# Row LSTM on one core: the even pixels' gate product moved to GpSimd, and a new written order of the half-step

## The chip, the core and the metric

The kernel runs on one core of a Trainium2 chip. The metric is device time in microseconds (us); the median of three runs of the kernel before is 2024.15 us (2023.83 to 2025.46).

## The reference

An input x of 8 images, 96 channels, 128 rows and 128 columns is group-normalised (32 groups). The normalised image goes through a masked 1x3 convolution to 384 gate channels. Then the rows are walked from top to bottom as time steps of a convolutional LSTM, and the result is added to x:

```python
def step(carry, row_in):
    h, c = carry
    ss = conv1d(h, W_ss, padding=1) + b_ss      # width 3, 96 -> 384 channels
    gates = ss + row_in
    f, i, o = sigmoid(gates[0]), sigmoid(gates[1]), sigmoid(gates[2])
    g = tanh(gates[3])
    c_new = f * c + i * g
    h_new = o * tanh(c_new)
    return (h_new, c_new), h_new
...
x = x + conv_lstm(group_norm(x))
```

All of it is float32. Row r+1 can't begin before h of row r is there, so the 128 rows are one long chain.

## The kernel before, in words

**Two chains.** The 8 images are two streams s of 4 images each. A half-step n is one row of one stream (n = 2 row + s), 256 half-steps in all. The streams don't depend on each other, so work of half-step n fills the waits of n-1. Rows come in blocks of R = 4.

**Statistics first.** The first 140 us or so read all of x and make means and scales (VectorE's bn_stats, ScalarE's sums). The loop over half-steps follows, from `do(n, PERIOD, by_lanes=True)` (L937).

**Products.** Columns are held as even and odd pixels, t = 0 and 1 (called a and b in the written order), 256 columns each for four images. The width-3 convolution is done with sums and differences of neighbours: `vs` = even + odd (L573), `vf` = odd - even (L585), both on VectorE with two SBUF inputs, and `vd`, the differences with the shifted neighbour (L589, GpSimd). The gate channels are three tiles A, B, C of 128: 96 rows of a sigmoid gate (A forget, B input, C output) and 32 rows of the tanh gate. Each tile has a PSUM bank of 512 columns, even and odd half. Eight banks go round. Products of the input's own convolution are P, Q, E (from `xs`), those of h are 1 (vs), 2 (vf), 0 and 3 (vd). In the loop TensorE works as two row groups of 64 rows, called lanes; each of 1, 2, 0, 3 is written twice, once for each lane, so a half-step has 33 products. Where two lanes write the same bank one after the other, a wait is put between them (`Lanes.wait`, L394).

**After the products.** 1 and 2 go to the two halves of the bank; ScalarE copies the first with the bias (`cp`, L508), VectorE writes their sum (`lo`, even, L512) and difference (`hi`, odd, L516) back; products 3, E and 0 are then added on top. A matmul on a bank waits for the last VectorE write to that bank, whichever half it is in. Then ScalarE does sigmoid (`si`, L527) and tanh (`ta`, L520), VectorE the forget product (`fg`, L532), the gate product i * g (`gt`, L537), the cell sum (`ce`, L547), ScalarE tanh of c (`th`, L552), VectorE the output h (`ou`, L560), from which vf (`F`) and vs (`S`) of the stream's next row come.

**GpSimd** makes vd (`D`, L589), adds h to x (`re`, L607), and prepares later rows: `own_image` widens one image's rows from `xr` to `xw` (L297), and makes the sum (L315) and the differences (L316) into `xs`; `normalise_shared` writes the rows shared with h's tile (L297 too). `vd` carries a manual wait for the last of `vf` and `vs`.

**What sets the order.** The engines' queues are filled by hand: the string `PERIOD` (L678) is read name by name for every half-step n, and each name issues one instruction in its engine's queue. A quote mark after a name means half-step n-1, two mean n-2, a plus n+1; `F'` and `S'` make the operands of n+1 from h of n-1; a small a or b at the end means the even or odd pixels alone. `W` stands for `prepare(n - 1)`: own image, shared rows and row loads (SP's queue) of the half-step before. `FIRST` (L629) is what the first eight half-steps prepare. Within an engine, work runs in this order only.

```python
PERIOD = (
    "2A hiC' siA' D'' 1B 1A taA' 2B fg' 3C' 1A 0C' re'' taB' 2A 2B EC' 1B cpA 0C' 2C W loA cpB "
    "3C' 1C siB' loB PB+ QA+ hiA taCb' 2C hiB taCa' 0A gtb' 1C siC' gta' EA 0B ceb' cpC 3A PA+ "
    "cea' thb' PC+ 3B loC tha' QC+ oub' EB oua' QB+ 3A F' 3B 0A S' 0B"
)
```

Of the kernel before, what the change touches and what calls it, by code (L numbers as in the profile page):

```python
# [8 lines left out]
AF = mybir.ActivationFunctionType  # L9
# [6 lines left out]
def strided(ap, offset, dims):  # L16

    return bass.AP(ap.tensor, ap.offset + offset, [ap.ap[0], *[list(d) for d in dims]])
# [3 lines left out]
def kernel(  # L22
# [32 lines left out]
    nc = tc.nc  # L55
    B, C, H, W = x.shape
    P = 128
    NH = 2
    BH = B // NH
    R = 4  # L60
    NB = H // R
    J = W // 2
# [53 lines left out]
    def pair(shape, name):  # L116
        return [
            [const.tile(shape, F32, tag=f"{name}{s}{i}", name=f"{name}{s}{i}") for i in range(2)]
            for s in range(NH)
        ]  # L120
# [5 lines left out]
    xs = pair([P, R, 3, BH, J], "xs")  # L126
# [4 lines left out]
    xw = [const.tile([P, R, W + 1], F32, tag=f"xw{i}", name=f"xw{i}") for i in range(2)]  # L131
# [29 lines left out]
    E = mybir.EngineType  # L161
# [147 lines left out]
            s * BH + j,  # L309
        )  # L310

    def combine(xw, n, total, differences):

        e, o = xw[:, 0:n, 0:J], xw[:, 0:n, J + 1 :]
        nc.gpsimd.tensor_add(total, e, o)  # L315
        nc.gpsimd.tensor_sub(  # L316
            differences,
            strided(xw[:, 0, :], 0, [(W + 1, n), (J, 2), (1, J)]),
            strided(xw[:, 0, :], J + 1, [(W + 1, n), (0, 2), (1, J)]),
        )  # L320

    def own_image(s, k, j):

        to = xs[s][k % 2]
        widen(nc.gpsimd, xw[0], 0, R, s, k, j, 0)
        combine(xw[0], R, to[:, :, 0, j, :], to[:, :, 1:3, j, :])

    def own_row(xw, s, r, lo=0, hi=BH):

        to = xs[s][0]  # L330
        combine(
            xw[:, lo:hi],
            hi - lo,
            to[:, r, 0, lo:hi],
            to[:, r, 1:3, lo:hi].rearrange("p t b j -> p b t j"),
        )
# [19 lines left out]
    HB = BH * J  # L356
    NT = NB * R
    last = NT * NH - 1
# [49 lines left out]
    class HalfStep:  # L408


        def __init__(self, n):
            self.n, (self.row, self.s) = n, divmod(n, NH)
            self.ps, self.m1, self.moving, self.done, self.gates, self.th = {}, {}, {}, set(), None, None
            self.started, self.images, self.halves, self.writer = set(), {}, {}, {}
            self.hx = hx[self.s][self.row // R % 2][:, self.row % R]
            self.xs = xs[self.s][self.row // R % 2][:, self.row % R]
            self.c = cs[self.s].rearrange("p t b j -> p (t b j)")
# [34 lines left out]
        def own(self, a, i):  # L452

            low = a == order["A"] or (a == order["C"] and (self.s == 0 or (self.n, i) == (1, 2)))
            rhs = self.xs[:, i].rearrange("p b j -> p (b j)")
            self.mm(a, i % 2, wo[i], rhs, slice(0, C2) if low else slice(C2, P))
# [63 lines left out]
            nc.scalar.activation(self.part(g, lo, hi, t), self.part(ps, lo, hi, t), AF.Tanh)  # L520


        def sigmoid(self, a):
            if self.row == 0 and a == 0:
                return
            gate = self.ps[a][0:C]
            nc.scalar.activation(gate, gate, AF.Sigmoid)  # L527

        def forget(self):
            f = self.ps[0][0:C]  # L530
# [3 lines left out]
        def gated(self, lo=0, hi=BH, t=None):  # L534
            to = self.g if self.row > 0 else self.c
            to, i, g = (self.part(ap, lo, hi, t) for ap in (to, self.ps[1][0:C], self.g))
            nc.vector.tensor_mul(to, i, g)  # L537


        def part(self, ap, lo, hi, t=None):  # L540
            ap = ap.rearrange("p (t b j) -> p t b j", t=2, b=BH)
            return ap[:, :, lo:hi] if t is None else ap[:, t, lo:hi]
# [44 lines left out]
        def shifted(self, lo=0, hi=BH):  # L587
            h = self.hx[:, 0, lo, :]
            diff = nc.gpsimd.tensor_sub(  # L589
                self.operand("vd", 2)[:, :, lo:hi],  # L590
                strided(h, 1, [(BH * JP - 1, 2), (JP, hi - lo), (1, J)]),
                strided(h, 0, [(BH * JP + 1, 2), (JP, hi - lo), (1, J)]),
            )
            if self.last.ins.engine != E.Pool:
                tc.add_manual_dep(
                    diff.ins,
                    self.last.ins.name,
                    mybir.DependencyInfo(
                        mybir.DependencyClass.Sync, mybir.DependencyReason.SCHED_ONLY
                    ),  # L600
                    reason="GpSimd starts when VectorE is done with both SBUF reads",
                )

        def residual(self):
            s, row = self.s, self.row
            xo = xt[s, row // R][0:C, :, row % R, :].rearrange("p b (j t) -> p t b j", t=2)
            (nc.gpsimd if 2 * row + s < last else nc.vector).tensor_add(xo, xo, self.h)  # L607

    def store(s, k, lo, hi):
        nc.sync.dma_start(  # L610
# [7 lines left out]
    SHARED = (((0, 0, R), (3, 0, 1)), ((1, 0, R),), ((2, 0, R),), ((3, 1, R),))  # L618
# [4 lines left out]
    def shared(s, k, *images):  # L623
        return [
            (normalise_shared, nc.gpsimd, s, k, *(j if isinstance(j, tuple) else (j, 0, R)))
            for j in images
        ]

    FIRST = [  # L629
        own(0, 0),  # L630
        own(0, 1),
        own(0, 2) + shared(0, 1, 0, 1),
        own(0, 3) + [(load_rows, 0, 2)] + shared(0, 1, 2, 3),
        own(1, 0, 1),
        own(1, 2) + shared(1, 1, 0, 1),
        own(1, 3) + [(load_rows, 1, 2)] + shared(1, 1, 2, 3),
        [(own_image, 0, 2, 0), (own_image, 1, 2, 0)],
    ]

    def work(n):  # L640
        if n < len(FIRST):
            return FIRST[n]
        row, s = divmod(n, NH)
        k, r = divmod(row, R)
        parts = []
        if r == R - 1 and k + 2 < NB:
            parts.append((own_image, s, k + 2, 0))
        elif r < R - 1 and k + 1 < NB:
            parts.append((own_image, s, k + 1, r + 1))
        if k + 1 < NB:  # L650
            parts += shared(s, k + 1, *SHARED[r])
        if r == R - 2 and k + 2 < NB:
            parts.append((load_rows, s, k + 2))
        return parts

    worked = set()

    def prepare(n):
        if n not in worked:
            worked.add(n)  # L660
            for part, *args in work(n):
                part(*args)

    def finish(n):
        prepare(n)
# [10 lines left out]


    PERIOD = (  # L678
        "2A hiC' siA' D'' 1B 1A taA' 2B fg' 3C' 1A 0C' re'' taB' 2A 2B EC' 1B cpA 0C' 2C W loA cpB "
        "3C' 1C siB' loB PB+ QA+ hiA taCb' 2C hiB taCa' 0A gtb' 1C siC' gta' EA 0B ceb' cpC 3A PA+ "  # L680
        "cea' thb' PC+ 3B loC tha' QC+ oub' EB oua' QB+ 3A F' 3B 0A S' 0B"
    )
    PIXELS = {"a": (0, BH, 0), "b": (0, BH, 1)}
    SPLIT = ("taC", "gt", "ce", "th", "ou")
    PARTS = {
# [5 lines left out]
    steps = {}  # L691

    def half_step(n):
        if n not in steps:
            steps[n] = HalfStep(n)
        return steps[n]

    def do(n, names, by_lanes=False):

        for name in names.split():  # L700
            if name == "W":
                prepare(n - 1)
                continue
            at = n
            for mark, offset in (("'", -1), ("+", 1), ("*", 2)):
                at += offset * name.count(mark)
                name = name.replace(mark, "")
            pixels = PIXELS[name[-1]] if name[:-1] in SPLIT and name[-1] in PIXELS else ()
            whole_name = name[:-1] if pixels else name
            tile_ = whole_name[-1] if whole_name[-1] in order else ""  # L710
            part = whole_name[: len(whole_name) - len(tile_)]

            if part in ("S", "F", "D"):
                at += NH
            if not 0 <= at <= last:
                continue
            step = half_step(at)
            if name in step.done or whole_name in step.done:
                continue
            if by_lanes and (part in OWN or part in H_PRODUCTS) and (  # L720
                at < last or part in ("P", "Q") or (part, order[tile_]) in step.halves
            ):
                if step.piece(part, order[tile_]):
                    step.done.add(name)
                continue
            step.done.add(name)
            getattr(step, PARTS[part])(*([order[tile_]] if tile_ else []), *pixels)
            if by_lanes and part == "re":
                finish(at)
# [13 lines left out]
    late = []  # L743
# [106 lines left out]
    n = m = 0  # L850
    for b in range(B):
# [7 lines left out]
        for k in range(QW // CH):  # L859
# [11 lines left out]
            if alone:  # L871
                i = list(shares).index(k)
# [25 lines left out]
    j = BH - 1  # L898
# [104 lines left out]
```

## Time and profile before

| | us |
|---|---|
| median of three runs | 2024.15 |
| profiled execution | 2027.04 |
| its span | 2025.2 |
| one half-step in the loop (vf to vf) | 7.33 |
| TensorE busy in the span | 1923.3 |
| VectorE busy | 1529.1 |
| ScalarE busy | 1494.9 |
| GpSimd busy | 1473.1 |

In the profile PE is TensorE (a matmul of 64 rows is two records of 0.38 us), PEld its weight load, DVE is VectorE, ACT is ScalarE, POOL is GpSimd, SP issues the DMAs. A line of the timeline gives start and length in us, engine, source line, operation, output and input, sizes, and a count where several equal instructions follow each other. Idle time before an instruction stands in brackets with what ended it. An engine's busy time is the time in which at least one of its instructions is running.

### The profile page before, as it was taken

How to read it: one execution, taken by the hardware profiler on the slowest of the kernel's cores; microseconds unless marked ns; L12 is line 12 of the kernel's file. 1: busy time of each engine (PE TensorE's matmuls, PEld its weight loads, DVE VectorE, ACT ScalarE, POOL GpSimd, SP SyncE). 2: the span in 40 equal slices, each digit the busy share in tenths (PEclk: the TensorE clock that was granted, in tenths of full speed). 3: DMA queues.
4: the chain of work that ended last, by engine and by line, in shares of the span. 5: the costliest groups of instructions: out<-in, count | busy, mean ns of one | idle time of the engine just before them, and what ended most of it. 6: DMA issues, size and time to landing. Idle time of an engine off the chain costs nothing.

```text
span 2025.2 us, 44842 instructions
## 1 busy us (share of the span) xinstructions
PE 1923.3 (95%) x16936; PEld 1831.0 (90%) x16936; DVE 1529.1 (76%) x3996; ACT 1494.9 (74%) x3161; POOL 1473.1 (73%) x1712
## 2 busy tenths in 40 slices
PE   0289999999999999999999999999999999999998
PEld 0178999999999999999999999999999999999997
DVE  5767777777777777777777777777777777777776
ACT  3776777777777777777777777777777777777776
POOL 3348777777777777777777777777777777777752
PEclk9989999999999999999999999999999999999999
DMA  9994333444334334433433443343344333434411
GB/s 374 424 310 100 98 103 91 112 115 104 82 89 113 92 101 115 113 83 82 110 95 95 116 116 95 79 100 96 93 116 116 96 82 96 107 92 106 116 33 32
DMA packets 103382, 237.11 MB, mean 117 GB/s; under 512 B 5952, under 2 KB 8896, under 8 KB 97280
## 3 DMA queue, kind: packets, MB, share of 16 engines
q1 hardware_dynamic: 103168, 234.25, 42.0%
q8 instruction: 135, 2.21, 0.5%
q14 instruction: 79, 0.65, 0.1%
HBM read 183.90 MB, written 50.33 MB: 116 GB/s over the span
## 4 chain that ended last, share of the span: by engine, by line
PE 93%; DMA 4%; ACT 2%; DVE 1%; issue 0%; SPq 0%; POOL 0%; DVEq 0%; POOLq 0%
PE ps L442 92%; DMA piece<-in_x_dram 3%; DMA xs<-in_x_dram 1%; ACT piece L216 1%; PE ps L174 0%; ACT piece L217 0%; DVE bst L876 0%; ACT hx L295 0%; ACT piece L295 0%; DVE hx L560 0%; ACT xs L216 0%; ACT xs L217 0%; SPq L864 0%; PE pv L251 0%; DVE ps L516 0%
## 5 line engine op out<-in xcount | busy, mean ns | idle before, releaser
L442 PE MATMUL ps<-vd,wl 64*128 64x256 f32 (+1 forms) x6096 | 1390.9, 379 | 0.3
L442 PEld LDWEIGHTS ps<-vd,wl 64*128 64x128 f32 (+1 forms) x6096 | 1028.4, 186 | 45.7 <-issue 2.4
L442 PE MATMUL ps<-vs,wm 64*128 64x256 f32 (+1 forms) x3052 | 775.1, 380 | 4.9 <-POOL vs L573 4.4
L442 PE MATMUL ps<-vf,wm 64*128 64x256 f32 (+1 forms) x3052 | 766.3, 377 | 0.0
L527 ACT ACTIVATE ps<-ps 96x512 f32<-96x512 f32 x766 | 441.6, 577 | 356.2 <-PE ps L442 348.1
L442 PE MATMUL ps<-xs,wx 64*128 64x256 f32 x3080 | 637.8, 377 | 11.1 <-POOL xs L315 11.1
L589 POOL TENSOR_TENSOR vd<-hx 128x512 f32<-128x512 f32 x257 | 266.7, 1038 | 388.5 <-PE ps L442 384.8
L442 PEld LDWEIGHTS ps<-xs,wx 64*128 64x128 f32 x3080 | 494.0, 187 | 14.2 <-POOL xs L315 11.6
L520 ACT ACTIVATE g<-ps 32x256 f32<-32x256 f32 (+1 forms) x1021 | 468.6, 482 | 26.7 <-PE ps L442 6.3
L442 PEld LDWEIGHTS ps<-vf,wm 64*128 64x128 f32 (+1 forms) x3052 | 475.4, 187 | 11.0 <-PE ps L442 0.4
L442 PEld LDWEIGHTS ps<-vs,wm 64*128 64x128 f32 (+1 forms) x3052 | 459.6, 186 | 21.6 <-POOL vs L573 5.4
L512 DVE TENSOR_TENSOR ps<-m,ps 128x256 f32<-128x256 f32 x768 | 326.0, 425 | 192.5 <-ACT m L508 182.0
L442 PE MATMUL ps<-xs,wt 64*128 64x256 f32 x1530 | 453.2, 377 | 0.6 <-DVE ps L516 0.6
L508 ACT ACTIVATE m<-ps,wl 128x256 f32<-128x256 f32 x766 | 361.6, 474 | 90.9 <-PE ps L442 84.3
L532 DVE TENSOR_TENSOR ps<-ps,c 96x512 f32<-96x512 f32 x254 | 176.8, 696 | 232.9 <-PE ps L442 226.9
L607 POOL TENSOR_TENSOR x<-x,hx 96x512 f32<-96x512 f32 x255 | 330.8, 1297 | 6.7 <-DVE hx L560 6.7
L516 DVE TENSOR_TENSOR ps<-m,ps 128x256 f32<-128x256 f32 x768 | 300.8, 422 | 1.3 <-PE ps L442 1.2
L442 PEld LDWEIGHTS ps<-xs,wt 64*128 64x128 f32 x1530 | 280.0, 186 | 12.8 <-DVE ps L516 1.0
L316 POOL TENSOR_TENSOR xs<-xw 128x512 f32<-128x512 f32 (+1 forms) x254 | 270.9, 1067 | 0.0
L297 POOL TENSOR_SCALAR hx<-x,rstd,nmr 32x384 f32<-32x384 f32 (+2 forms) x312 | 225.8, 724 | 33.2 <-DMA x<-in_x_dram 1.1
L297 POOL TENSOR_SCALAR xw<-xr,rstd,nmr 128x512 f32<-128x512 f32 x252 | 205.6, 816 | 7.1 <-DVE nmr L289 6.5
L537 DVE TENSOR_TENSOR g<-ps,g 96x256 f32<-96x256 f32 x507 | 189.0, 413 | 3.8 <-ACT g L520 3.8
(91 smaller groups left out, 1223.1 us busy)
## 6 DMA issues: line engine op xcount, KB each, us to landing
xr<-in_x_dram SPq DMA_DIRECT2D x124, 512.0 KB, 6.4
x<-in_x_dram SPq DMA_DIRECT2D x63, 768.0 KB, 6.1
out_dram<-x SPq DMA_DIRECT2D x62, 768.0 KB, 4.6
xs<-in_x_dram SPq DMA_DIRECT2D x30, 1024.0 KB, 12.3
piece<-in_x_dram SPq DMA_DIRECT2D x16, 1024.0 KB, 12.3
x<-in_x_dram SPq DMA_DIRECT2D x62, 256.0 KB, 3.2
xs<-in_x_dram SPq DMA_DIRECT2D x4, 512.0 KB, 8.7
out_dram<-x SPq DMA_DIRECT2D x2, 576.0 KB, 3.7
```

The costliest lines, as they stand in the source:

```text
L297: return engine.tensor_scalar(dst, src, scale, shift, ALU.mult, ALU.add)
L316: nc.gpsimd.tensor_sub(differences, strided(xw[:, 0, :], 0, [(W + 1, n), (J, 2), (1, J)]), strided(xw[:, 0, :], J + 1, [(W + 1, n), (0, 2) ...
L442: made = nc.tensor.matmul(self.ps[a][:, bass.ts(half, HB)][:, cols], weights[rows, bass.ts(a, P)], rhs[rows, cols], start=new, stop=False, ...
L508: nc.scalar.activation(self.m1[a], m1, AF.Identity, bias=column)
L512: nc.vector.tensor_add(self.ps[a][:, 0:HB], self.m1[a], self.ps[a][:, HB:])
L516: nc.vector.tensor_sub(hi, self.m1[a], hi)
L520: nc.scalar.activation(self.part(g, lo, hi, t), self.part(ps, lo, hi, t), AF.Tanh)
L527: nc.scalar.activation(gate, gate, AF.Sigmoid)
L532: nc.vector.tensor_mul(f, f, self.c)
L537: nc.vector.tensor_mul(to, i, g)
L589: diff = nc.gpsimd.tensor_sub(self.operand("vd", 2)[:, :, lo:hi], strided(h, 1, [(BH * JP - 1, 2), (JP, hi - lo), (1, J)]), strided(h, 0, ...
L607: (nc.gpsimd if 2 * row + s < last else nc.vector).tensor_add(xo, xo, self.h)
```

## The change

Five edits:

1. The sigmoid of tile B is done in two halves. The odd half stays in PSUM; the even half is written to a new SBUF tile `i`. The gate product of the even pixels reads that tile and runs on GpSimd; the odd pixels' product stays on VectorE.
2. `PERIOD` is written anew. Sigmoid A is issued at the end of its own half-step, tanh B, the first half of sigmoid B and tanh A ahead of the copies; odd A comes directly after even A; products P and E of later use are ahead of 0A.
3. What a half-step prepares is split in three places: U (first half-steps only), V (shared rows, right after the residual) and W (own image and row loads). W now stands after the gate product `gta'`, so on GpSimd the own image comes after it.
4. The residual on GpSimd gets the same manual wait for the stream's next vs as vd has.
5. The first eight half-steps do five of their shared-row normalisations on ScalarE, and two own images of stream 1 are cut in three parts that go to different half-steps (`apart`, `LATER`).

```diff
-        def sigmoid(self, a):
+        def sigmoid(self, a, lo=0, hi=BH, t=None):
             if self.row == 0 and a == 0:
                 return
-            gate = self.ps[a][0:C]
-            nc.scalar.activation(gate, gate, AF.Sigmoid)
+            gate = self.part(self.ps[a][0:C], lo, hi, t)
+            if t == 0:
+                self.even_input = self.tile("i", (C, HB))
+                to = self.even_input.rearrange("p (b j) -> p b j", b=BH)
+            else:
+                to = gate
+            nc.scalar.activation(to, gate, AF.Sigmoid)
...
-            nc.vector.tensor_mul(to, i, g)
+            if t == 0 and self.even_input is not None:
+                i = self.even_input.rearrange("p (b j) -> p b j", b=BH)
+                nc.gpsimd.tensor_mul(to, i, g)
+            else:
+                nc.vector.tensor_mul(to, i, g)
...
-            if self.last.ins.engine != E.Pool:
+            self.hold(diff)
+
+        def hold(self, made):
+            if self.last is not None and self.last.ins.engine != E.Pool:
                 tc.add_manual_dep(
-                    diff.ins,
+                    made.ins,
...
-            (nc.gpsimd if 2 * row + s < last else nc.vector).tensor_add(xo, xo, self.h)
+            made = (nc.gpsimd if 2 * row + s < last else nc.vector).tensor_add(xo, xo, self.h)
+            following = steps.get(self.n + NH)
+            if self.n < last and following is not None:
+                following.hold(made)
...
+    def on_scalar(s, k, *images):
+        return [(normalise_shared, nc.scalar, s, k, j, 0, R) for j in images]
+
+    def apart(s, k, j):
+        to = xs[s][k % 2]
+        return (
+            (widen, nc.gpsimd, xw[1], 0, R, s, k, j, 0),
+            (add_pixels, xw[1], R, to[:, :, 0, j, :]),
+            (subtract_pixels, xw[1], R, to[:, :, 1:3, j, :]),
+        )
+
+    spread = apart(1, 1, 0)
     FIRST = [
-        own(0, 0),
-        own(0, 1),
-        own(0, 2) + shared(0, 1, 0, 1),
-        own(0, 3) + [(load_rows, 0, 2)] + shared(0, 1, 2, 3),
-        own(1, 0, 1),
-        own(1, 2) + shared(1, 1, 0, 1),
-        own(1, 3) + [(load_rows, 1, 2)] + shared(1, 1, 2, 3),
-        [(own_image, 0, 2, 0), (own_image, 1, 2, 0)],
+        ([], [], own(0, 0)),
+        ([], [], own(0, 1)),
+        ([], [], own(0, 2)),
+        (on_scalar(0, 1, 0), [spread[0]], own(0, 3) + [(load_rows, 0, 2)]),
+        (on_scalar(0, 1, 1), list(spread[1:]), own(1, 1)),
+        (on_scalar(0, 1, 2) + on_scalar(1, 1, 2), shared(0, 1, 3), own(1, 2)),
+        (on_scalar(1, 1, 3), shared(1, 1, 0, 1), own(1, 3) + [(load_rows, 1, 2)]),
+        ([], [], [(own_image, 0, 2, 0)]),
     ]
+    LATER = dict(zip((11, 13, 15), apart(1, 2, 0)))
...
+        early, late = shared(s, k + 1, *SHARED[r]) if k + 1 < NB else [], []
+        if n in LATER:
+            early.append(LATER[n])
+        ahead, image = (k + 2, 0) if r == R - 1 else (k + 1, r + 1)
+        if ahead < NB:
+            late.append((own_image, s, ahead, image))
         if r == R - 2 and k + 2 < NB:
-            parts.append((load_rows, s, k + 2))
-        return parts
+            late.append((load_rows, s, k + 2))
+        return [], early, late
...
     PERIOD = (
-        "2A hiC' siA' D'' 1B 1A taA' 2B fg' 3C' 1A 0C' re'' taB' 2A 2B EC' 1B cpA 0C' 2C W loA cpB "
-        "3C' 1C siB' loB PB+ QA+ hiA taCb' 2C hiB taCa' 0A gtb' 1C siC' gta' EA 0B ceb' cpC 3A PA+ "
-        "cea' thb' PC+ 3B loC tha' QC+ oub' EB oua' QB+ 3A F' 3B 0A S' 0B"
+        "2A 1B 1A U taB' 2B 3C' siBa' 1A 0C' taA' 2A 2B EC' fg' 1B cpA D'' re'' V 0C' 2C siBb' "
+        "loA 3C' cpB 1C hiA PB+ QA+ taCb' loB 2C taCa' PA+ gtb' 1C gta' W siC' EA hiB PC+ ceb' 0A "
+        "cpC cea' 0B 3A thb' loC 3B tha' QB+ oub' 3A oua' EB 0A F' 0B QC+ S' siA 3B hiC"
     )
-    SPLIT = ("taC", "gt", "ce", "th", "ou")
+    SPLIT = ("taC", "siB", "gt", "ce", "th", "ou")
```

`combine` is only cut into `add_pixels` and `subtract_pixels`, which it calls; on the built program's GpSimd queue a half-step reads vd, residual, shared rows, gate product, widen, sum, differences.

More of the change, by code (lines that the diff above doesn't have):

```diff
@@ L310, in widen, with add_pixels, subtract_pixels @@
         )
-    def combine(xw, n, total, differences):
-        e, o = xw[:, 0:n, 0:J], xw[:, 0:n, J + 1 :]
-        nc.gpsimd.tensor_add(total, e, o)
+    def add_pixels(xw, n, total):
+        nc.gpsimd.tensor_add(total, xw[:, 0:n, 0:J], xw[:, 0:n, J + 1 :])
+    def subtract_pixels(xw, n, differences):
         nc.gpsimd.tensor_sub(
@@ L320, in combine @@
         )
+    def combine(xw, n, total, differences):
+        add_pixels(xw, n, total)
+        subtract_pixels(xw, n, differences)
     def own_image(s, k, j):
@@ L414, in __init__ @@
             self.started, self.images, self.halves, self.writer = set(), {}, {}, {}
+            self.even_input = self.last = None
             self.hx = hx[self.s][self.row // R % 2][:, self.row % R]
@@ L644, in work, with prepare @@
         k, r = divmod(row, R)
[L645 to L651, printed above, removed]
+        early, late = shared(s, k + 1, *SHARED[r]) if k + 1 < NB else [], []
[4 more added lines that the diff above has]
+            late.append((own_image, s, ahead, image))
         if r == R - 2 and k + 2 < NB:
-            parts.append((load_rows, s, k + 2))
-        return parts
+            late.append((load_rows, s, k + 2))
+        return [], early, late
     worked = set()
[L658 to L662, printed above, removed]
+    def prepare(n, parts=(0, 1, 2)):
+        for i in parts:
+            if (n, i) not in worked:
+                worked.add((n, i))
+                for part, *args in work(n)[i]:
+                    part(*args)
     def finish(n):
@@ L700, in do @@
         for name in names.split():
-            if name == "W":
-                prepare(n - 1)
+            if name in "UVW":
+                prepare(n - 1, range("UVW".index(name) + 1))
                 continue
```

## The prediction

> **What bounds the kernel now.** I read the page's busy shares and chain first, then the busy time by stretches of 200 us, then the timeline of one half-step engine by engine.
>
> ```profile
> PE 1923.3 (95%) x16936; PEld 1831.0 (90%) x16936; DVE 1529.1 (76%) x3996; ACT 1494.9 (74%) x3161; POOL 1473.1 (73%) x1712
> ...
> PE 93%; DMA 4%; ACT 2%; DVE 1%; issue 0%; SPq 0%; POOL 0%; DVEq 0%; POOLq 0%
> ```
> ```profile
> 400.00:600.00 200.00, 200.00 (x1803) 192.26 (x1802) 152.94 (x408) 150.44 (x327) 154.24 (x170) 1.00 0.39 98
> ```
>
> TensorE looks full, but busy is the union of two row-group lanes: one lane may sit idle unseen. In the timeline a lane takes a record every 0.216 us (1004.12, 1004.34, 1004.55, 1004.77). A half-step has 33 products of two records each, over two lanes: 33 x 0.216 = 7.12 us. It takes 7.33 (vf at 1000.97 and 1008.30). The 0.21 missing is seen here, VectorE's timeline and then TensorE's:
>
> ```profile
> 1000.97 0.42 DVE L585 TENSOR_TENSOR vf<-hx 128x256 f32<-128x256 f32 x1
> 1001.31 0.42 DVE L573 TENSOR_TENSOR vs<-hx 128x256 f32<-128x256 f32 x1
> ...
> 1004.39 0.90 DVE L512 TENSOR_TENSOR ps<-m,ps 128x256 f32<-128x256 f32 x2 [0.70 <-ACT m L508]
> 1005.20 0.76 DVE L516 TENSOR_TENSOR ps<-m,ps 128x256 f32<-128x256 f32 x2
> ...
> 1007.52 0.74 DVE L560 TENSOR_TENSOR hx<-ps,th 96x256 f32<-96x256 f32 x2
> 1008.30 0.42 DVE L585 TENSOR_TENSOR vf<-hx 128x256 f32<-128x256 f32 x1
> ```
> ```profile
> 1004.99 0.63 PE L442 MATMUL ps<-xs,wx 64*128 64x256 f32 x4
> 1005.42 0.59 PE L442 MATMUL ps<-vf,wm 64*128 64x256 f32 x2
> 1005.77 0.45 PE L442 MATMUL ps<-vd,wl 64*128 64x256 f32 x1
> ```
>
> The vd product (0A) waits for odd A (L516, first of the pair, done at 1005.62), which stands behind even A and even B. One lane is empty from 1005.46 to 1005.77. So the bound is a loop: last product on A, copy A, even A, even B, odd A, 0A. TensorE alone would be 3% faster.
>
> GpSimd's timeline over the same half-step shows when the SBUF port is free:
>
> ```profile
> 1001.90 1.04 POOL L589 TENSOR_TENSOR vd<-hx 128x512 f32<-128x512 f32 x1 [1.55 <-PE ps L442]
> 1002.90 1.30 POOL L607 TENSOR_TENSOR x<-x,hx 96x512 f32<-96x512 f32 x1
> 1004.18 0.81 POOL L297 TENSOR_SCALAR xw<-xr,rstd,nmr 128x512 f32<-128x512 f32 x1
> 1005.07 0.65 POOL L315 TENSOR_TENSOR xs<-xw 128x256 f32<-128x256 f32 x1
> 1005.67 1.07 POOL L316 TENSOR_TENSOR xs<-xw 128x512 f32<-128x512 f32 x1
> 1006.85 0.82 POOL L297 TENSOR_SCALAR hx<-x,rstd,nmr 32x512 f32<-32x512 f32 x1
> ```
>
> It is done at 1007.67, 0.63 us before the next vf. The idle 1.55 before vd is put down to a TensorE product; vd also waits for vs, which ends 0.17 before it (1001.73 to 1001.90). That gap is what keeps vf and vs alone on the port. Early in the run it is missing (timelines of VectorE, GpSimd, TensorE at 160 us):
>
> ```profile
> 160.45 0.43 DVE L585 TENSOR_TENSOR vf<-hx 128x256 f32<-128x256 f32 x1
> 160.79 1.29 DVE L573 TENSOR_TENSOR vs<-hx 128x256 f32<-128x256 f32 x1
> ```
> ```profile
> 160.46 1.34 POOL L316 TENSOR_TENSOR xs<-xw 128x512 f32<-128x512 f32 x1
> ```
> ```profile
> 162.13 0.70 PE L442 MATMUL ps<-vs,wm 64*128 64x256 f32 x3
> ```
>
> vf wins the port, the subtraction L316 waits for it (1.34 for 1.07) and then keeps vs out until 162.08, 1.63 after vf's start where 0.76 is usual. Products on vs start at 162.13. The same happens at 200.66, and the next vf comes 8.11 later, not 7.33.
>
> **What the Trainium skill says.** "SBUF — State Buffer", "Who interferes with whom": a VectorE instruction with two SBUF inputs contends with a GpSimd instruction that reads SBUF; the first takes the port for its whole length, the other blocks. The trace agrees, with the 1.29 us above. One SBUF input beside PSUM doesn't contend: agreed, L315 keeps to 0.64 under VectorE's PSUM operations. "GPSIMD Engine Reference", "Engine selection": two-input elementwise work is about twice as slow on GpSimd as on VectorE. Here it is 0.64 against 0.42 for 128x256, and I use the trace.
>
> **The change part by part.**
>
> Order of products: 0A moves from 19th to 23rd of 33, and odd A stands right behind even A. Odd A comes one VectorE slot (0.34) earlier and 0A four product slots (4 x 0.216 = 0.86) later, so the 0.31 wait goes. Worth up to 0.21 per half-step.
>
> Sigmoid B in two halves: ScalarE gets two 96x256 at about 0.41 (L552's size) for one 96x512 of 0.58, +0.2; it has over 1.5 us free per half-step. Nothing on the path.
>
> Even gate product (L537, first in time for the odd pixels, second for the even): VectorE loses one 0.33 slot; GpSimd gains 96x256, not shown there: its nearest row is L315, 0.64; upper end 0.73, the longer of its two 128x256 differences before the loop; I take 0.64. It waits for the even half of tanh C. Behind it on GpSimd stand, by the built program's order, the own image (L297, L315, L316) and then the next vd. For it waits the cell sum of the even pixels, and behind that on VectorE the output, vf and vs.
>
> The own image is so moved from before the gate to after it. GpSimd now runs vd, residual, shared rows, [wait] gate, own image: 1.04+1.30+0.81+0.64+2.6 = about 6.4 us, and vd can't start until 0.17 after vs ended. Counted from vs's end (0):
> - 1B starts at 0.05 (162.08 to 162.13). From it to the second 3C' are 13 products: six rounds of two lanes, 6 x 0.43, and the last of 0.59: 3.18. Sum 3.23.
> - tanh C in two halves 0.65 and a 0.04 wait: 3.92. A GpSimd wait is 0.08 (L297's end at 1004.99 to L315 at 1005.07): gate 4.00 to 4.64.
> - Even cell, tanh, output 3 x 0.41, and four waits of 0.035: vf is ready at 6.01, or up to 0.14 later if the odd pixels' instructions hold it: 6.08.
> - GpSimd: own image starts at 4.60 (its back-to-back overlap is 0.04), the subtraction L316 1.49 later (1004.18 to 1005.67): 6.09, to end at 7.16.
>
> vf and the subtraction arrive within 0.1 us of each other: the picture of 160.45. vs ends 1.63 after vf's start: 6.08+1.63 = 7.71. If instead the subtraction is first, vf ends 0.28 after it (so at 152.84, in the same trace) and vs 0.34 after that: 6.09+1.07+0.62 = 7.78. TensorE's record after a wait took 0.45 for 0.38, so I take 7.75 per half-step. The gate's own start carries both sides, so the meeting repeats in every half-step that prepares an image.
>
> Bounds: vs-to-product wait 0.15 as at odd A, gate 0.73, vf at its latest: 7.71+0.10+0.09+0.07 = 7.97. Below: vf at 6.01 and no restart: 7.64.
>
> Residual after vs: it stands behind vd, which already waits for vs: nothing. The row loads of x on SP's queue follow the own image, so go some 2 us later; they land in 6.4 us and are used two half-steps on: hidden, with some 6 us to spare. First rows: five normalisations go to ScalarE. vf at 152.84 to 208.77 takes 55.9 us for seven half-steps, 7.99 each.
>
> Sum: (2006.1-208.8)/7.334 = 245 half-steps, of which the last 7 prepare no image. 238 x (7.75-7.334) = +99; 7 x (7.12-7.33) = -1.5; first seven at 7.75, -1.7. Together +96. The profiled execution took 2027.04 (span 2025.2), so 2123; it lies 2.9 over the median of 2024.15, which gives 2120.
>
> **Rivals.**
> - TensorE-bound, faster. vs slips in ahead of the waiting subtraction. At 1448.99 it did, where a GpSimd instruction had started 0.09 before it; at 160.79 and 201.00 GpSimd had started 0.33 and 0.30 before and won. Here the lead is 0.34 minus the 0.01 by which the subtraction starts after vf: 0.33, and 0.26 if vf comes earliest. The turn lies between 0.09 and 0.30. Then the half-step is 7.12: 245 x -0.214 = -52, 1972. Against: vd has to wait for the delayed subtraction, though the move of 0A gives it over 2 us.
> - Part of it: the meeting occurs in every other half-step, or vs loses only about half: 238 x (0.208-0.107) = +24, 2048.
> - Worse: both blocks, slow restarts and new lane waits (EB stands two places behind 3B on the other lane): 8.05, 238 x 0.72 = +171, 2195.
>
> **Chances.** Forecast 0.68 (7.64 to 7.97: 2094 to 2173), TensorE-bound 0.16, in part 0.08, worse 0.08. The range runs from the partial case to the worse one, 2045 to 2195, leaving out the fast case and edges. 0.2% is about what a measurement can tell from no change: faster 0.17, same 0.01, slower 0.82.
>
> **What would show it.** Right: vf to vf near 7.75; vs about 1.3 us long beside an image subtraction (L318 in the changed file) of 1.3; idle TensorE ahead of ps<-vs naming VectorE's vs; odd A no longer released late. Wrong: vs at 0.42 and half-steps of 7.12 (the port doesn't decide), or gate products starting far from 4.00 after vs.

## The result and the profile after

| | before | after |
|---|---|---|
| median, us | 2024.17 (2023.83 to 2025.46, 4 runs) | 2178.03 (2177.32 to 2181.18, 4 runs) |
| ratio, 95% interval | | 1.0762 (1.0743 to 1.078) |
| span of the profiled execution | 2025.2 | 2179.1 |
| one half-step, vf to vf, median in the loop | 7.33 | 7.945 |
| the same, mean of 238 half-steps of the loop | 7.336 | 7.996 |

The change makes the kernel 7.6% slower. The page of the changed kernel, busy shares and the chain that ended last:

```profile
PE 1991.3 (91%) x16936; PEld 1713.8 (79%) x16936; DVE 1692.6 (78%) x3743; ACT 1514.6 (70%) x3419; POOL 1712.8 (79%) x1960
...
DVE 54%; PE 24%; DMA 9%; ACT 5%; POOL 4%; issue 2%; SPq 0%; POOLq 0%; DVEq 0%
```

The chain was TensorE's at 93%; now VectorE has 54% of it and TensorE 24%. VectorE runs 253 instructions fewer than before and is busy 163 us more: an instruction that is blocked counts as busy, as the long vs below show. The stretches of 200 us show TensorE idle in the steady loop, where it was busy for 200.00 of 200 (the columns are PE, PEld, DVE, ACT and POOL, each with its instructions, then clock, DMA share and GB/s):

```profile
400.00:600.00 200.00, 191.19 (x1658) 163.96 (x1654) 159.03 (x352) 140.15 (x327) 167.35 (x183) 1.00 0.37 93
```

The groups by line show which instructions grew (the count, then busy us and mean ns of one, then the idle us before them and what ended most of it):

```profile
L450 PEld LDWEIGHTS ps<-vs,wm 64*128 64x128 f32 (+1 forms) x3052 | 454.5, 186 | 199.0 <-DVE vs L590 168.9
...
L318 POOL TENSOR_TENSOR xs<-xw 128x512 f32<-128x512 f32 (+1 forms) x254 | 329.1, 1296 | 0.1
L552 POOL TENSOR_TENSOR g<-i,g 96x256 f32<-96x256 f32 x253 | 183.2, 724 | 171.5 <-ACT g L528 170.1
L590 DVE TENSOR_TENSOR vs<-hx 128x256 f32<-128x256 f32 (+1 forms) x254 | 302.1, 1189 | 0.0
```

vs takes 1.189 us on average, the subtraction of the own image 1.296. Unblocked they took 0.42 and 1.07 in the kernel before. The weight load of the products on vs idles 199.0 us, 168.9 of it until vs ends. Both orders of the meeting are in the timeline, VectorE first and then GpSimd:

```profile
574.43 0.43 DVE L602 TENSOR_TENSOR vf<-hx 128x256 f32<-128x256 f32 x1
574.77 1.29 DVE L590 TENSOR_TENSOR vs<-hx 128x256 f32<-128x256 f32 x1
...
582.37 1.35 DVE L602 TENSOR_TENSOR vf<-hx 128x256 f32<-128x256 f32 x1
```
```profile
572.22 0.73 POOL L552 TENSOR_TENSOR g<-i,g 96x256 f32<-96x256 f32 x1 [0.87 <-ACT g L528]
572.93 0.82 POOL L297 TENSOR_SCALAR xw<-xr,rstd,nmr 128x512 f32<-128x512 f32 x1
573.83 0.64 POOL L314 TENSOR_TENSOR xs<-xw 128x256 f32<-128x256 f32 x1
574.43 1.34 POOL L318 TENSOR_TENSOR xs<-xw 128x512 f32<-128x512 f32 x1
576.20 1.04 POOL L606 TENSOR_TENSOR vd<-hx 128x512 f32<-128x512 f32 x1 [0.43 <-DVE vs L590]
...
582.37 1.07 POOL L318 TENSOR_TENSOR xs<-xw 128x512 f32<-128x512 f32 x1
```

At 574.43 vf has the port first: the subtraction is stretched to 1.34 and keeps vs out until 576.06. At 582.37 the subtraction has it first and keeps its 1.07, and vf is stretched to 1.35 instead. 225 of the 254 vs on VectorE and 18 vf are longer than 1 us. TensorE's timeline starts again only behind the stretched vs:

```profile
576.11 0.70 PE L450 MATMUL ps<-vs,wm 64*128 64x256 f32 x4 [0.34 <-DVE vs L590]
576.65 0.38 PE L450 MATMUL ps<-vf,wm 64*128 64x256 f32 x1
```

When no own image is left to prepare, the next half-steps are short and vs is 0.42 again, in the same program (VectorE's timeline near the end):

```profile
2101.59 1.29 DVE L590 TENSOR_TENSOR vs<-hx 128x256 f32<-128x256 f32 x1
...
2109.19 0.43 DVE L602 TENSOR_TENSOR vf<-hx 128x256 f32<-128x256 f32 x1
2109.53 0.42 DVE L590 TENSOR_TENSOR vs<-hx 128x256 f32<-128x256 f32 x1
...
2116.41 0.43 DVE L602 TENSOR_TENSOR vf<-hx 128x256 f32<-128x256 f32 x1
```

From vf to vf these take 7.22 to 7.29 us, against 7.945 in the loop.

### The profile page after: what moved, and what is told of

It is laid out like the page before. It is cut to its first block, busy times and chain, and to the rows that moved or that the text cites. A ratio compares the mean times of both kernels' runs of the same rounds, so it can differ in the third digit from the quotient of the medians.

```text
span 2179.1 us, 45093 instructions
## 1 busy us (share of the span) xinstructions
PE 1991.3 (91%) x16936; PEld 1713.8 (79%) x16936; DVE 1692.6 (78%) x3743; ACT 1514.6 (70%) x3419; POOL 1712.8 (79%) x1960
## 4 chain that ended last, share of the span: by engine, by line
DVE 54%; PE 24%; DMA 9%; ACT 5%; POOL 4%; issue 2%; SPq 0%; POOLq 0%; DVEq 0%
PE ps L450 24%; DVE vs L590 12%; DVE ps L520 11%; DVE c L564 7%; DVE ps L524 7%; DVE hx L577 7%; DVE vf L602 5%; ACT m L516 5%; DVE g L554 4%; DMA xs<-in_x_dram 4%; DMA out_dram<-x 3%; DMA x<-in_x_dram 2%; POOL x L627 1%; POOL hx L297 1%; DVE bst L912 1%
## 5 line engine op out<-in xcount | busy, mean ns | idle before, releaser
L450 PE MATMUL ps<-vd,wl 64*128 64x256 f32 (+1 forms) x6096 | 1299.2, 376 | 0.3
L450 PEld LDWEIGHTS ps<-vd,wl 64*128 64x128 f32 (+1 forms) x6096 | 1008.0, 186 | 57.9 <-issue 1.7
L450 PE MATMUL ps<-xs,wx 64*128 64x256 f32 x3080 | 722.9, 377 | 11.8 <-POOL xs L314 11.1
L450 PEld LDWEIGHTS ps<-vs,wm 64*128 64x128 f32 (+1 forms) x3052 | 454.5, 186 | 199.0 <-DVE vs L590 168.9
L540 ACT ACTIVATE ps<-ps 96x512 f32<-96x512 f32 x766 | 387.6, 506 | 270.4 <-PE ps L450 262.0
L450 PEld LDWEIGHTS ps<-xs,wx 64*128 64x128 f32 x3080 | 474.6, 187 | 44.2 <-POOL xs L314 11.5
L450 PE MATMUL ps<-xs,wt 64*128 64x256 f32 x1530 | 479.7, 394 | 0.6 <-DVE ps L524 0.5
L318 POOL TENSOR_TENSOR xs<-xw 128x512 f32<-128x512 f32 (+1 forms) x254 | 329.1, 1296 | 0.1
L552 POOL TENSOR_TENSOR g<-i,g 96x256 f32<-96x256 f32 x253 | 183.2, 724 | 171.5 <-ACT g L528 170.1
L590 DVE TENSOR_TENSOR vs<-hx 128x256 f32<-128x256 f32 (+1 forms) x254 | 302.1, 1189 | 0.0
L450 PEld LDWEIGHTS ps<-xs,wt 64*128 64x128 f32 x1530 | 260.3, 186 | 23.9 <-DVE ps L524 0.9
```

The lines of the kernel that those rows point to most:

```text
L318: nc.gpsimd.tensor_sub(differences, strided(xw[:, 0, :], 0, [(W + 1, n), (J, 2), (1, J)]), strided(xw[:, 0, :], J + 1, [(W + 1, n), (0, 2) ...
L450: made = nc.tensor.matmul(self.ps[a][:, bass.ts(half, HB)][:, cols], weights[rows, bass.ts(a, P)], rhs[rows, cols], start=new, stop=False, ...
L540: nc.scalar.activation(to, gate, AF.Sigmoid)
L552: nc.gpsimd.tensor_mul(to, i, g)
L590: self.last = engine.tensor_add(self.operand("vs")[:, 0, lo:hi], e, o)
```

## The experiments

The port theory: the gate pushes the own image back until its subtraction meets vf and vs, and this meeting is the loss. The load theory: GpSimd has too much to do, wherever it stands. The gate theory: the gate product is slower on GpSimd and lies on the path of h. The order theory: the new order of the products, or sigmoid B in halves, costs the time. All edits are against the changed kernel unless said otherwise; the page's line numbers shift by a few in some.

### The subtraction left out (e3_no_subtraction)

The differences of the own image are not made for blocks 4 and later, and TensorE multiplies old data in their place, so this kernel computes something else.

```diff
-    combine(xw[0], R, to[:, :, 0, j, :], to[:, :, 1:3, j, :])
+    combine(xw[0], R, to[:, :, 0, j, :], to[:, :, 1:3, j, :] if k < 4 else None)
```

> The changed kernel with the own image's differences (L318) left out from the fifth block of rows on (k of 4 and more); TensorE multiplies old data in their place, and everything else is issued as before. About 214 half-steps are without it. Port theory: in these vs takes 0.42 and the half-step is 7.12 to 7.23: 2178 - 214 x 0.75 = about 2018. Gate theory and order theory: nothing that they name is touched, 7.9, 2178. Load theory: GpSimd has 1.3 less of 6.7 us, so about 7.2 too; it is told apart by the run with the shared rows on ScalarE.

2050.91 us, ratio 1.0134 (1.0101 to 1.0166). The median half-step is 7.232, as expected, and not the 7.12 of the prediction's floor. Gate, order and halved sigmoid are all as in the changed kernel, so the loss of the usual half-step is none of theirs. The total is not as expected: 52.5 us lie in longer half-steps. Some 11 us of these are half-steps that still make the differences; some 40 us are at the start of blocks. GpSimd's timeline there:

```profile
624.32 1.29 POOL L628 TENSOR_TENSOR x<-x,hx 96x512 f32<-96x512 f32 x1
626.10 1.36 POOL L297 TENSOR_SCALAR hx<-x,rstd,nmr 32x512 f32<-32x512 f32 x2 [0.49 <-DMA x<-in_x_dram]
```

The shared rows stand right behind the residual, and they wait for x, whose load waits for the store of the block before, which waits for the residual. In the changed kernel, where each half-step is slow anyway, the longer half-steps are 11.8 us in all. The kernel before had its shared rows at the end of GpSimd's half-step and waited 1.1 us in all.

### The subtraction behind vs (e10_subtraction_after_vs)

Nothing is left out; the differences are issued after `S'` and held until that vs has ended, as vd is.

```diff
-        "... QC+ S' siA 3B hiC"
+        "... QC+ S' X siA 3B hiC"
...
+    def subtract_held(n, differences):
+        made = subtract_pixels(xw[0], R, differences)
+        following = steps.get(n + 2)
+        if following is not None:
+            following.hold(made)
```

> The changed kernel with one thing moved: the own image's differences (L318 in the changed kernel) are issued after vs, and wait for it by the same manual wait as vd; so GpSimd runs differences, vd, residual, shared rows, gate, widen, sum. All work is kept. Port theory: no meeting, vs at 0.42; GpSimd's round from vs to gate is 0.17+1.07+1.04+1.25+0.80 = 4.3, and the half-step about 7.3: 238 x 0.65 = 155 less, 2023, plus waits of the shared rows for x at the blocks' first rows, as in the run without differences (some 25 to 50): 2040 to 2075. If the gate's place behind tanh C, and not the differences' place, is what costs: 7.9, 2178.

2090.41 us, ratio 1.032 (1.0303 to 1.0338). GpSimd and then VectorE:

```profile
703.48 0.64 POOL L314 TENSOR_TENSOR xs<-xw 128x256 f32<-128x256 f32 x1
704.92 1.07 POOL L318 TENSOR_TENSOR xs<-xw 128x512 f32<-128x512 f32 x1 [0.80 <-DVE vs L597]
705.94 1.04 POOL L613 TENSOR_TENSOR vd<-hx 128x512 f32<-128x512 f32 x1
```
```profile
704.08 0.43 DVE L609 TENSOR_TENSOR vf<-hx 128x256 f32<-128x256 f32 x1
704.42 0.42 DVE L597 TENSOR_TENSOR vs<-hx 128x256 f32<-128x256 f32 x1
```

Made to wait 0.80 us, the subtraction costs less than when it doesn't: the half-step falls from 7.945 to 7.365, with the same work on GpSimd. So the meeting on the port costs at least 0.58 us per half-step, 238 x 0.58 = 138 us where the whole loss is 154. The longer half-steps at the start of blocks grew here too, to 63.8 us, which is why the total missed what was expected. They are waits for x only in part, as e12 below shows.

### Less work on GpSimd (e4_shared_on_scalar)

The shared rows go to ScalarE behind tanh A; gate and own image stay where they are.

```diff
+        early = [(part, nc.scalar, *rest) for part, _, *rest in early]
-        "... re'' V 0C' ... 3B tha' QB+ ..."
+        "... re'' 0C' ... 3B tha' V QB+ ..."
```

> The changed kernel with the shared rows' normalisation (about 0.8 us of GpSimd's 6.7 per half-step) on ScalarE after tanh of the cell; the gate still comes behind residual, and the own image behind the gate. Port theory: the gate's start is set by tanh C and not by GpSimd's work, so the own image meets vf and vs as before: 7.9 per half-step, 2160 to 2180 (the lower end if the few waits for x in shared rows go). Load theory: GpSimd is lighter by 0.8, half-step 7.2, about 2000. Gate and order theories: no change, 2178.

2175.23 us, ratio 1.0748 (1.0717 to 1.0779), half-step 7.940. GpSimd has some 0.9 us less in each half-step, and the time is nearly that of the changed kernel. The load theory falls: the own image starts when the gate ends, and the gate when tanh C ends, however idle GpSimd is before.

### The own image ahead of the gate (e2_image_before_gate)

```diff
-        "... D'' re'' V 0C' ... gta' W siC' ..."
+        "... D'' re'' V W 0C' ... gta' siC' ..."
```

> The changed kernel with the own image moved ahead of the gate product on GpSimd (vd, residual, shared rows, own image, gate). Port theory with its loop: no meeting, vs at 0.42, but now the gate comes last on GpSimd and the loop is vs, vd, residual, shared rows, own image, gate, cell, tanh, output, vf, vs: 0.17+1.04+1.26+0.79+2.56+0.73+1.48+0.76 = 8.8 per half-step, 2178 + 238 x 0.85 = about 2380. Load theory: the work is the same in sum, 7.95, 2178. Order theory: 2178. A view that the meeting alone matters, wherever the gate is: 7.2, 2000.

2439.05 us, ratio 1.2051 (1.2016 to 1.2086), half-step 8.927. vs is not blocked any more, but the gate is late. The waits of 400 to 1800 us (who waited for whom: us in total, times, longest):

```profile
DVE c L564 <- POOL g L552: 282.4, 152, 2.4
...
PEld ps L450 <- DVE vf L602: 229.2, 151, 2.1
```

vd, residual, shared rows and own image are some 5.7 us that follow vs, and the cell sum waits 282.4/152 = 1.86 us for the gate behind them. In this order the gate is late; in the changed kernel's, the subtraction.

### The gate back on VectorE (e1_gate_on_vector)

```diff
-                nc.gpsimd.tensor_mul(to, i, g)
+            nc.vector.tensor_mul(to, i, g)
```

> The changed kernel with the even gate product back on VectorE and both halves of sigmoid B left in PSUM; order of the products, place of the own image and all else as changed. Port theory (the own image's differences meet vf and vs on the SBUF port because they stand behind the gate): GpSimd is done well before vf, vs takes 0.42, and the half-step is bound elsewhere; the products PC+ now wait for both gate products on VectorE, so 7.3 rather than 7.12: 2178 - 238 x 0.63 = about 2030. Order theory (the new order of the products costs by itself): stays near 7.9, 2140 to 2178. Load theory (GpSimd has too much work in sum): falls too, to about 7.2, near 2000. Gate theory (the slower gate product lies on the path of h): falls by the 0.3 that it is slower and the waits around it, 7.5 or so: 2075.

Sigmoid B stays in PSUM as well. 2080.91 us, ratio 1.0282 (1.0252 to 1.0312); half-step 7.450, 18 vs over 1 us. Undoing the move takes 97 of the 154 us back, so the new order alone isn't the main loss. Nor is it the gain that I had expected: with the gate on VectorE the half-step is 7.450 against 7.33 before. Another 24 us are longer half-steps with waits for x. The two waits:

```profile
PEld ps L450 <- DVE g L545: 50.7, 185, 0.4
POOL hx L297 <- DMA x<-in_x_dram: 46.2, 45, 2.2
```

In the new order a weight load waits 0.27 us in each half-step for VectorE's gate products. I take these to free the bank that the next products write; that was read from the order, not tried.

### Shared rows later, and everything in its place (e12, e5, e11)

e12 is e10 with the shared rows one row later, so that x has landed:

```diff
-    SHARED = (((0, 0, R), (3, 0, 1)), ((1, 0, R),), ((2, 0, R),), ((3, 1, R),))
+    SHARED = ((), ((0, 0, R), (3, 0, 1)), ((1, 0, R),), ((2, 0, R),))
...
+        if r == 0 and k > 1:
+            early = shared(s, k, (3, 1, R))
```

> As the run with the differences after vs, and in addition the shared rows of the next block are prepared one row later (nothing of the next block in the first row of a block; the last image's rows in the first row of their own block). If the irregular half-steps at the first row of each block are waits for the load of x, which follows the store and so the residual: they go, 7.3 throughout, 2178 - 238 x 0.65 - 12 = 2012. If they have another cause, the time stays where the run before it stands.

2064.27 us, ratio 1.0196 (1.018 to 1.0211). No wait for x is listed any more, and the time falls by 26 us: about so much were these waits worth. The other 37 us of longer half-steps are still there. They are now in each block's second row, where two pieces of shared rows (32x512 and 32x128) stand ahead of the gate: such half-steps take 7.92 to 7.94 where others take 7.36. In e10 the same two pieces were in the block's first row, hidden among the waits for x. VectorE's cell sum waits for the gate:

```profile
DVE c L571 <- POOL g L559: 75.9, 187, 0.9
```

e5 keeps the gate on GpSimd in the order vd, own image, gate, residual, with the shared rows on ScalarE:

```diff
+        early = [(part, nc.scalar, *rest) for part, _, *rest in early]
...
-        "... cpA D'' re'' V 0C' ... gta' W siC' ... 3B tha' QB+ ..."
+        "... cpA D'' W 0C' ... gta' re'' siC' ... 3B tha' V QB+ ..."
```

> As the run with all moved, but the shared rows keep their row: in a block's first row they follow the load of x. The load waits for the store, the store for the residual, which now comes 3 us later, so ScalarE's queue should wait for x up to 4 us in such half-steps, two of every eight, with sigmoid A behind it: 1996 plus 60 x 2 to 4 = 2110 to 2230. If the waits for x are of no consequence: 1996.

2071.51 us, ratio 1.0233 (1.0212 to 1.0253): faster than expected, half-step 7.281, and 61.8 us of longer half-steps, nearly all at the start of blocks, where ScalarE now waits for x. e11 is e5 with e12's later rows:

> The changed kernel, its gate product still on GpSimd, with GpSimd's order vd, own image, gate, residual; the shared rows on ScalarE after tanh of the cell and one row later. All work is kept. Port theory: own image done before tanh C, residual done 0.2 before vf, no meeting; TensorE then sets 7.12 plus the 0.11 of the lane wait of EB, 7.23: 2178 - 238 x 0.715 - 12 = 1996, under the kernel before. Load theory (two-input work on GpSimd is the cost, wherever it stands) or gate theory (a gate product of 0.72 for 0.41 on the path of h): not under 2024.

2022.43 us, ratio 0.9992 (0.9983 to 1.0). The loss is gone, with the gate on GpSimd, but the gain that I expected isn't there: half-steps of 7.23 alternate with some of 7.3 to 7.64, mean 7.317. The wait that I took for the cause:

```profile
DVE vf L602 <- ACT hx L295: 31.3, 96, 0.4
```

### Which rows the next vf reads (e13, e14, e15, e16)

e13 spreads the pieces so that no vf reads one of the same half-step; single rows (32x128) go to GpSimd between own image and gate. e14 is e13 with the gate on VectorE. The edit to the shared rows:

```diff
+    SHARED = ((), ((0, 0, R),), ((1, 0, R),), ((2, 1, R),))
+    BETWEEN = ((), ((3, 0, 1),), ((3, 1, 2),), ((2, 0, 1),))
...
```

> Gate still on GpSimd, GpSimd in the order vd, own image, gate, residual, as in the run with all moved; the shared rows are spread so that no half-step has more than one piece on ScalarE, none of these is what the next vf reads, and single rows (32x128) go on GpSimd between the own image and the gate. Theory (the change's loss is the port meeting plus the place of the shared rows; with both gone TensorE's loop of 33 products with one lane wait, 7.23 us, is left everywhere): median half-step 7.23 to 7.28, mean under 7.29, against 7.317 in the run with all moved, which is some 238 x 0.06 = 15 us less: 1998 to 2012 us, faster than before by 0.6 to 1.3%. Rival (ScalarE's 0.85 us for a piece delays the next half-step wherever it stands, or the piece on GpSimd delays the gate): mean stays at 7.31 or more, 2018 to 2035 us.

> The same kernel with the even gate product back on VectorE (sigmoid B left in PSUM): what the move of the gate alone is worth once GpSimd no longer meets VectorE. Theory (VectorE's stretch from even A to vf becomes the loop when it has the gate, as in the run with the gate on VectorE and the change's order, 7.45 us a half-step, less the waits of TensorE for both gates): median half-step 7.33 to 7.45, 2022 to 2055 us, 15 to 45 us slower than its pair. Rival (the gate is hidden on either engine): within 5 us of its pair.

e13: 2023.51 us, ratio 0.9994 (0.9986 to 1.0003): the rival came true. vf waits for nothing, but half-steps with a single row are 7.35:

```profile
DVE c L564 <- POOL g L552: 30.0, 119, 0.5
```

A row of 32x128 takes 0.46 us on GpSimd, more than half of the 0.81 of 32x512, and doesn't fit in the gap.

e14: 2057.18 us, ratio 1.0164 (1.0148 to 1.0179), half-step 7.450, and one wait again:

```profile
PEld ps L450 <- DVE g L545: 49.4, 187, 0.3
```

Against its pair the gate on GpSimd is worth 33.7 us. So in this order the move itself, with its halved sigmoid B, is a gain, once the own image doesn't follow it.

e15 puts the single rows behind the residual, where GpSimd idles 1.15 us (the edit against e13):

```diff
-    BETWEEN = ((), ((3, 0, 1),), ((3, 1, 2),), ((2, 0, 1),))
+    BETWEEN = ((), ((3, 0, 1),), ((2, 0, 1),), ((3, 1, 2),))
...
-        "... cpA D'' W X 0C' ... gta' re'' siC' ..."
+        "... cpA D'' W 0C' ... gta' re'' X siC' ..."
```

> As the run with spread rows, but the single rows on GpSimd come behind the residual instead of between the own image and the gate (and rows 0 and 1 of images 2 and 3 change places over the half-steps, so that none is read by the next vf). In the run with spread rows such a piece took 0.46 us and some 0.1 between it and its neighbours, in a gap of 0.35 to 0.5, and VectorE's second cell addition waited 0.33 us for the gate in the half-steps with one: median 7.35 there, 7.07 and 7.23 where there was none. GpSimd idles 1.15 us behind the residual. Theory (the delay of the gate is the whole excess over TensorE's 7.23): half-steps of 7.23 throughout, mean 7.22 to 7.26, 238 x 0.05 to 0.09 = 12 to 21 us less, 2002 to 2012 us, 0.6 to 1.1% faster than before. Rival (ScalarE's piece of 0.85 us ahead of sigmoid A is as late, and holds the half-step at 7.3): 2018 to 2024 us.

2057.37 us, ratio 1.0162 (1.0148 to 1.0176). Neither theory: the edit made a new wait.

```profile
ACT hx L295 <- POOL hx L297: 138.3, 142, 1.2
```

ScalarE's piece goes into the same tile hx as GpSimd's, and waits 0.97 us for it although the two are different images. In e13, where GpSimd's row came earlier, no such wait is listed. I had put GpSimd's row ahead of ScalarE's in the written order without asking who writes that tile next.

e16 is e11 with nothing but other pieces: all on ScalarE, the two rows that the next vf reads two half-steps earlier (the edit against e11).

```diff
-    SHARED = ((), ((0, 0, R), (3, 0, 1)), ((1, 0, R),), ((2, 0, R),))
+    SHARED = ((), ((0, 0, R), (3, 0, 2)), ((1, 0, R), (2, 0, 1)), ((2, 1, R),))
-            early = shared(s, k, (3, 1, R))
+            early = shared(s, k, (3, 2, R))
```

> As the run with all moved, with the shared rows still all on ScalarE behind tanh A, but rows 0 and 1 of images 3 and 2, which the next two vf read, two half-steps earlier: so no vf reads a piece that is normalised in the same half-step. In the run with all moved, vf waited 0.39 us for such a piece in two of eight half-steps and 0.26 in two more, and the half-steps with two pieces (1.38 us) were 7.23 all the same. Theory (these waits are the whole excess of its mean, 7.31, over TensorE's loop): 7.23 in every half-step, 238 x 0.08 = 19 us less, 2000 to 2008 us, 0.8 to 1.2% faster than before. Rival (with two pieces in four of eight half-steps, sigmoid A and through it the gate come late): mean 7.30 or more, 2018 to 2030 us.

2010.19 us (2009.33 to 2011.13), ratio 0.9929 (0.9915 to 0.9942): faster than both kernels, a little less than expected. The mean half-step is 7.263: of the 0.087 by which e11 stood over 7.23, 0.054 went, and what holds the rest stays open. The stretch of 400 to 600 us shows TensorE busy throughout again, with more records in it than before (1820 against 1803); GpSimd's timeline has gate and residual last in its half-step and vd held by vs alone:

```profile
400.00:600.00 200.00, 200.00 (x1820) 194.74 (x1819) 144.30 (x383) 181.94 (x402) 151.37 (x166) 1.00 0.41 99
```
```profile
700.48 0.64 POOL L314 TENSOR_TENSOR xs<-xw 128x256 f32<-128x256 f32 x1
701.08 1.07 POOL L318 TENSOR_TENSOR xs<-xw 128x512 f32<-128x512 f32 x1
702.71 0.73 POOL L552 TENSOR_TENSOR g<-i,g 96x256 f32<-96x256 f32 x1 [0.56 <-ACT g L528]
703.39 1.31 POOL L627 TENSOR_TENSOR x<-x,hx 96x512 f32<-96x512 f32 x1
705.82 1.04 POOL L606 TENSOR_TENSOR vd<-hx 128x512 f32<-128x512 f32 x1 [1.12 <-DVE vs L590]
```

## Why the prediction was right

Its direction, its mechanism and its range of 2045 to 2195 hold; the likeliest time, 2120, is 58 us low. The narrower band that it gave its own mechanism, 2094 to 2173, is missed by 5 us: the measured time lies in the part of the range that was left open for the worse rival. By its own steps:

**The bound before.** 0A waiting for odd A goes with the new order, as said. But TensorE alone doesn't reach 7.12. Where nothing else is in the way (e3, the end of the changed kernel, e16) the half-step is mostly 7.22 to 7.29. There one record in each half-step is 0.48 us instead of 0.38 (TensorE in e16):

```profile
704.40 0.59 PE L450 MATMUL ps<-vd,wl 64*128 64x256 f32 x2
704.62 0.48 PE L450 MATMUL ps<-xs,wt 64*128 64x256 f32 x1
```

It is product E on B, which waits for 3B on the other lane, three places ahead of it in the new order (the prediction said two): the lane wait that the prediction gave to its worst rival alone. No run took this wait away, so that it makes the whole 0.1 is argued. Other products follow the other lane on their bank at the same distance, the second 2C for one, and have no long record; why this one does stays open. So the gain of 0.21 was too much: with the gate on GpSimd and everything in its place the half-step comes to 7.23 to 7.26, against 7.33 before, and with the gate on VectorE (e1) the new order loses 0.12.

**The gate.** It starts 4.11 us after vs's end (4.00 said) and takes 0.725; the prediction took 0.64 from the nearest row and had 0.73 as its upper end. "GPSIMD Engine Reference", "Engine selection", in the Trainium skill has two-input elementwise work about twice as slow on GpSimd; here it is 0.725 against 0.41, 1.77 times, nearer to that than the row that I used (0.64 against 0.42).

**The meeting.** vf starts 1.48 us after the gate ends (1.37 to 1.51 said), at the same moment as the subtraction, and vs ends 1.633 after vf's start (1.63 said). "SBUF — State Buffer", "SBUF: two separate sides", in the Trainium skill says that the operation which starts first holds the shared port for its whole length and the other waits; both timelines above agree, with vs at 1.29 and vf at 1.35. That it repeats in nearly every half-step was said and holds: 225 vs and 18 vf of 254 each are stretched.

**The half-step: the terms that were mis-sized.** With vf first the steps gave 7.71, 7.75 was taken, and 7.945 was measured, inside the bound of 7.97. From 7.71 on: the first product on vs to the end of the second 3C' 3.29 for 3.18 (+0.11), the gate (+0.085), gate to vf 1.48 for 1.44 (+0.04), which gives 7.945. The 0.11 is TensorE's restart behind the wait: the next round starts 0.54 after 576.11, and each later one 0.43 after the last. The kernel before shows the same 0.54 behind its blocked vs, from 162.13 to 162.67. The prediction counted six rounds of 0.43, and gave the restart the 0.04 from 7.71 to 7.75. Against the 7.75 all this is 238 x 0.195 = 46 us.

**The sum.** The median is 7.945, the mean 7.996: longer half-steps of 11.8 us, most of them at the start of blocks, where the shared rows wait for x. The prediction did not see these waits. It gave the new place of the shared rows, right behind the residual, no cost. The whole: 238 x (7.996 - 7.336) = +157; the first seven half-steps +0.7, where -1.7 was said; the last seven -0.7, where -1.5 was said; and the loop begins 3.2 us earlier (second vf on VectorE at 149.60 instead of 152.84), which the prediction did not list and which no run here explains. That is 153.8, against 153.9 between the spans. Of the 58 us that the likeliest time is low, 46 are the half-step and 12 the waits for x; the rest cancels. The row loads on SP's queue delayed nothing that shows, as said; the hold on the residual was not tried by itself.

**The rivals.** vs did not slip in ahead of the subtraction (0.33 us of lead was said to be too much, and was). "In part" fails on the count of blocked vs. The worse one named slow restarts and the lane wait, and both exist, at 0.1 each; its half-step of 8.05 did not come.

## What to carry to other kernels

Work moved to an idle engine must be judged by what stands behind it in that engine's queue: here what the moved product pushed back met a VectorE pair on the SBUF port, and 0.58 us of each half-step went when that one subtraction was held. Waiting on purpose for the pair's end was cheaper than meeting it. When a stall is removed, ask what it hid: waits for x made up most of 11.8 us in the slow version, and moving the rows later took 26 us (e10 to e12) and 49 us (e5 to e11) off faster ones.

## What I had not expected of the hardware

- A blocked VectorE operation ends 0.28 to 0.29 us after the GpSimd one, in all 243 cases of the changed kernel: the subtraction ended at 575.77, vs at 576.06.
- Small pieces are dear on GpSimd: the normalisation of 32x512 took 0.81 us, 32x384 0.69, 32x128 0.46 (means of e1). On ScalarE 32x512 took 0.85 and 32x256 0.61 (means of e13).
- GpSimd's gate product of 96x256 (0.725) is slower than its sum of 128x256 (0.64), with fewer partitions; what makes the difference was not tried.
